# A Mamba layer and a mixture of experts in one kernel: weights fetched apart from token rows, the scan one projection later, counts per block of 512, the optional blocks ahead of the last two

## The chip, the cores and the metric

The kernel runs on one core of one Trainium2 chip. The metric is the device time of one execution in microseconds. TensorE (PE) does the matmuls, VectorE (DVE), ScalarE (ACT) and GpSimd (POOL) everything elementwise, and transfers are issued from the queues of SyncE (SP), ACT and POOL. PEld is PE's weight load, which overlaps its matmuls.

## The reference

4096 tokens of 256 features pass through two layers, each with a residual and a layer norm. The first is a Mamba block (512 inner channels, convolution over 4 tokens, 16 states, a scan over all tokens), the second a mixture of 8 experts that sends each token to one of them.

```python
xz = input_tensor @ W_in                      # 256 -> 2 * 512
conv_in, gated = xz[..., :512], xz[..., 512:]
convolved = silu(causal_conv(conv_in, conv_w) + conv_b)
x_dbl = convolved @ W_x                       # delta, B, C
delta = softplus(x_dbl[..., :1])
h = exp(delta * A) * h + delta * B * convolved[..., :16]     # scan over tokens
y = sum(h * C) + convolved * D_param
x = layernorm(x + (y * silu(gated)) @ W_out)

e = argmax(x @ Wr.T + br)                     # one expert for each token
x = layernorm(x + relu(x @ W1[e].T + b1[e]) @ W2[e].T + b2[e])
```

## The kernel before

**The Mamba part** goes in NB = 8 chunks of TB = 512 tokens, JT = 4 tiles of 128 each. Step k of the main loop issues the eight projections of chunk k (`project(k, 0)` to `project(k, 7)`, tile `pm`, L477, 128 columns of W_in each), and between them the later stages of the chunks a = k-1, b = k-2 and c = k-3. ACT evicts the first four to `xc` and `acc` (L484, L486), DVE convolves (L490), and ACT applies silu (L482, L493). Chunk a gets `gauge` (px, L502), `gauge_out` (pxo, and a long DVE chain to `sr`, L515 to L546), `look_out` and `scan` (pt, L554, then exp, scan and `hC`, to L565). Chunk b gets `gate` (py, L572), `project_out` in four tiles (po, L612) and `choose`, in which the expert is found and the tokens of each expert are counted (`earlier`, L666). Chunk c gets `rank` (pr, L677 and L680: each token's place within its expert), `blocks_of` and `place` (rowh, colh and pz, L703 to L717: lists of the tokens by place).

**The table.** Sorted by expert, the tokens make blocks of 128. At most NSB = 39 blocks are needed; the first SURE = 37 always run. `blocks_of` calls `table` after chunks 2, 4, 5 and 7, which set up blocks 0 to 4, 5 to 12, 13 to 16 and 17 to 38. It computes which expert a block belongs to (`widx`, L294) and returns a function `lookup`. This one reads the token numbers out of the lists (pi, L306; `tidx`, L313) and is called later, by `tokens_of`, once the lists are placed.

**An expert block** (`blocks`, a generator that yields after each quarter) has these pieces. `fetch` issues two indirect transfers from POOL: the 128 token rows `xg` (L352, 128 KB, four buffers) and the expert's whole weights `we` (L357, 2.23 MB, three buffers), for blocks up to AHEAD = 2 ahead. `turn` transposes the rows (pg L376, copy `xgT` on DVE, L380). `hidden` makes each half of the hidden layer (ph L392; relu by ACT, L400, for the first, and by DVE, L402, for the second). `close` does the second matmul in halves (pe L414), adds `xs` = xg + b2 (L421) and the result (`r`, L423), the layer norm (L217 to L224) and an indirect write from POOL (`out`, L426). The generator `quarters` runs over blocks 0 to 36, and `expert(n)` takes n quarters of it. `fill` says how many after each projection in the steps k = 6 and 7; behind the loop calls of `expert` alternate with the last stages, and then the rest runs. The last two blocks stand in a conditional (L840) that compares a number read from the table; the profiled execution doesn't take it.

**What sets the order.** PE's order is that of the code, written by hand. The other engines' order is the framework's scheduler's. PSUM banks are shared by tag: three for pm, px and ph (`mm`), two for transposes and small results (`tr`), and those for py, po and pe (`o`). The weights of the router are prepared by `router_weights` (pw L336, pwo L344), called in step 0.

Of the kernel before, what the change touches and what calls it, by code (L numbers as in the profile page):

```python
# [33 lines left out]
F32 = mybir.dt.float32  # L34
# [4 lines left out]
ALU = mybir.AluOpType  # L39
# [40 lines left out]
def mamba_moe(  # L80
# [53 lines left out]

    load(0)
    win = const.tile([P, DC, 2 * DI], F32, name="win")
    for at in (slice(0, DI), slice(DI, 2 * DI)):
        nc.sync.dma_start(win[:, 0, at], W_in[0:P, at])
        nc.scalar.dma_start(win[:, 1, at], W_in[P : 2 * P, at])
        if at.start == 0:  # L140
            cw = const.tile([P, CC, KC], F32, name="cw")
            nc.scalar.dma_start(cw, conv_w.rearrange("(c p) k -> p c k", p=P))
            cb = const.tile([P, CC], F32, name="cb")
            nc.sync.dma_start(cb, conv_b)
# [83 lines left out]

    index = {}

    taken = const.tile([P, NE], F32, name="taken")

# [4 lines left out]
    def table(b0, nb, columns, rows, early):  # L239
# [52 lines left out]
        nc.vector.tensor_scalar(eb, eb, float(NE - 1), float(P), ALU.min, ALU.mult)  # L292
        widx = const.tile([P, nb], I32, name=f"widx{b0}")
        nc.vector.tensor_scalar(widx, eb, part, None, ALU.add)  # L294
        if early:

            left = small("left", [NE])
            nc.vector.tensor_scalar(left, starts, -1.0, float(nb * P), ALU.mult, ALU.add)
            nc.vector.scalar_tensor_tensor(left, left, 0.0, whole, ALU.max, ALU.min)
            nc.vector.tensor_tensor(taken, taken, left, ALU.add)  # L300

        def lookup():

            pi = bank("tr", f"pi{b0}", 2)
            for h in range(LH):
                nc.tensor.matmul(  # L306
                    pi[:, 0:nb], lhsT=lists[:, h * P : (h + 1) * P], rhs=pick[:, h, :],
                    start=(h == 0), stop=(h == LH - 1),
                )
            half = small("half", [nb])  # L310
            nc.vector.tensor_scalar(half, pi[:, 0:nb], 0.0, -float(T + 1), ALU.is_gt, ALU.mult)
            tidx = const.tile([P, nb], I32, name=f"tidx{b0}")
            nc.vector.scalar_tensor_tensor(tidx, pi[:, 0:nb], float(T), half, ALU.add, ALU.add)  # L313
            for b in range(nb):
                index[b0 + b] = rows, widx[:, b : b + 1], tidx[:, b : b + 1]

        return lookup

# [28 lines left out]
                )  # L347
        nc.scalar.copy(wout[:, :, D : D + NE], pov)

    def fetch(b):  # L350
        xg = m3.tile([P, D], F32, tag="xg", name=f"xg{b}", bufs=4)
        nc.gpsimd.indirect_dma_start(  # L352
            out=xg, out_offset=None, in_=x1d[0 : index[b][0], :],
            in_offset=bass.IndirectOffsetOnAxis(ap=index[b][2], axis=0),
        )
        we = m3.tile([P, WROW], F32, tag="we", name=f"we{b}")
        nc.gpsimd.indirect_dma_start(  # L357
            out=we, out_offset=None, in_=experts,
            in_offset=bass.IndirectOffsetOnAxis(ap=index[b][1], axis=0),
        )  # L360
        return xg, we

    fetched, turned, hid, open_ = {}, {}, {}, {}

    current = 0

    def prefetch(b):
        for ahead in range(b, min(b + AHEAD, (SURE if b < SURE else NSB) - 1) + 1):
            if ahead in index and ahead not in fetched:
                fetched[ahead] = fetch(ahead)  # L370

    def turn(b):

        px = bank("tr", f"pg{b}", 2)
        for dc in range(DC):
            nc.tensor.transpose(  # L376
                px[:, dc * P : (dc + 1) * P], fetched[b][0][:, dc * P : (dc + 1) * P], ident
            )
        turned[b] = m2.tile([P, DC * P], F32, tag="xgT", name=f"xgT{b}")
        nc.vector.tensor_copy(turned[b], px[:, 0 : DC * P])  # L380

    def hidden(b, half):
        we, xgT = fetched[b][1], turned[b]
        if half == 0:
            hid[b] = m2.tile([P, FC, P], F32, tag="hT", name=f"hT{b}")
        hT = hid[b]
        ph = bank("mm", f"ph{b}_{half}")
        fcs = range(half * FC // 2, (half + 1) * FC // 2)
        for n, fc in enumerate(fcs):
            for dc in range(DC):  # L390
                at = dc * FF + fc * P
                nc.tensor.matmul(  # L392
                    ph[:, n * P : (n + 1) * P], lhsT=we[:, at : at + P],
                    rhs=xgT[:, dc * P : (dc + 1) * P],
                    start=(dc == 0), stop=(dc == DC - 1),
                )
        for n, fc in enumerate(fcs):
            bias = we[:, OB + fc : OB + fc + 1]
            if half == 0:
                nc.scalar.activation(hT[:, fc, :], ph[:, n * P : (n + 1) * P], AF.Relu, bias=bias)  # L400
            else:
                nc.vector.tensor_scalar(  # L402
                    hT[:, fc, :], ph[:, n * P : (n + 1) * P], bias, 0.0, ALU.add, ALU.max
                )

    def close(b, half):
        xg, we = fetched[b]
# [18 lines left out]
        nc.gpsimd.indirect_dma_start(  # L426
            out=out, out_offset=bass.IndirectOffsetOnAxis(ap=index[b][2], axis=0),
            in_=y[:, 0, :], in_offset=None, bounds_check=T - 1, oob_is_err=False,
        )

    def blocks(*span):

        nonlocal current
        turn_next = True
        for b in range(*span):
            current = b
            prefetch(b)
            if turn_next:
                turn(b)
            hidden(b, 0)  # L440
            yield
            hidden(b, 1)
            yield
            turn_next = b + 1 not in fetched
            if not turn_next:
# [195 lines left out]
    def choose(i):  # L641
# [19 lines left out]
        nc.vector.tensor_reduce(best, lg, AX.X, ALU.max)  # L661
        oh = a2.tile([P, JT, NE], BF16, tag="oh", name=f"oh{i}")
        nc.vector.tensor_tensor(oh, by_token(back), by_expert(best), ALU.is_equal)
        for j in range(JT):
            at = i * JT + j
            nc.vector.tensor_tensor(  # L666
                earlier[:, at + 1, :], earlier[:, at, :], oh[:, j, :], ALU.add
            )
        st[i]["oh"], st[i]["best"] = oh, best

    def rank(i):
# [5 lines left out]
        nc.tensor.matmul(  # L677
            prv, lhsT=trib, rhs=oh.rearrange("p j e -> p (j e)"), start=True, stop=False
        )
        nc.tensor.matmul(  # L680
            prv, lhsT=oneb,
            rhs=earlier[:, i * JT : (i + 1) * JT, :].rearrange("p j e -> p (j e)"),
            start=False, stop=True,
        )
        rk = a2.tile([P, JT, NE], F32, tag="rk", name=f"rk{i}")
        nc.vector.tensor_tensor(
# [37 lines left out]

    def blocks_of(i):

        done = len(index)
        if i + 1 in EARLY:
            lookups[i] = table(done, EARLY[i + 1] - done, (i + 1) * JT, (i + 1) * TB, True)
# [8 lines left out]
    def have(i):  # L738
        return 0 <= i < NB
# [5 lines left out]
    for k in range(NB):  # L745
# [53 lines left out]
    tokens_of(c - 1)  # L799
    expert(2)  # L800
    gauge_out(a)
    expert()
# [84 lines left out]
```

## Time and profile before

| what | us |
|---|---|
| median of 3 runs (lowest, highest) | 566.27 (565.71, 566.81) |
| the profiled execution's own time | 564.27 |
| its span in the profile | 562.4 |
| PE busy | 507.1 |
| DVE, ACT, POOL busy | 349.1, 226.0, 174.3 |
| bytes moved by DMA | 106.92 MB, of which 91.65 MB on POOL's software queue |
| mean granted PE clock | 0.963 of full speed |

By stage, PE busy of the time: 20.2 of the first 30.0 us; 26.9 of 30 to 60; 111.9 of 60 to 180; 13.1 of 180 to 200, where the first expert block starts; 92.4 of 200 to 300 and 55.8 of 300 to 360, where expert blocks and the last Mamba stages are mixed; 179.6 of 360 to 540, expert blocks alone; 7.2 of the last 22.4.

The profile's page gives each engine's busy time and its state in 40 slices of the span. The waits are the idle times of an engine, sorted by what ended them. The timeline gives single instructions with their start and duration; in square brackets stands how long the engine was idle before, and what released it. Records of matmuls overlap, so their lengths don't add up. A line number is that of the kernel before.

### The profile page before, as it was taken

The page shows a single profiled execution, that of the slowest core. Times are in us where ns is not written, and L with a number is a line of the kernel's source. Part 1 is how long each engine was busy: PE and PEld are TensorE (multiplying, and loading weights), DVE is VectorE, ACT ScalarE, POOL GpSimd, SP SyncE. Part 2 cuts the span into 40 slices and gives each one's busy share as a digit, 9 for nine tenths or more (in the row PEclk, how much of TensorE's full clock was granted, in tenths as well). Part 3 has the DMA queues.
Part 4 walks back from the last instruction along what each step waited for, and adds up shares of the span by engine and source line. Part 5 has one row for each costly group of instructions (what it writes and reads, how often), then busy time and mean ns, then how long its engine had stood idle before and what let it go on. Part 6 is the DMA issues. An engine that isn't in the chain of part 4 may idle for free. (4 is left out here: it accounts for less than half of the span.)

```text
span 562.4 us, 7855 instructions
## 1 busy us (share of the span) xinstructions
PE 507.1 (90%) x2754; PEld 385.9 (69%) x2754; DVE 349.1 (62%) x1171; ACT 226.0 (40%) x462; POOL 174.3 (31%) x191
## 2 busy tenths in 40 slices
PE   4897999898989599989969898999999999999990
PEld 1533454545454377567659787998999999999980
DVE  0446879786898827876858968444544445554440
ACT  2358576776676526575523211111111111111110
POOL 2000303333244531332432512323333444444210
PEclk9699999998999789989989999999999999999996
DMA  9110103030309704604545856888999999989900
GB/s 264 41 38 1 38 1 112 2 112 1 113 1 361 272 4 169 233 10 169 180 141 195 305 210 226 316 318 314 352 336 340 343 345 343 336 337 358 339 28 0
DMA packets 22729, 106.92 MB, mean 190 GB/s; under 512 B 4222, under 2 KB 12929, under 8 KB 17954
## 3 DMA queue, kind: packets, MB, share of 16 engines
q0 software_dynamic: 8880, 91.65, 43.7%
q1 hardware_dynamic: 10928, 12.85, 7.3%
q10 hardware_dynamic: 2882, 1.93, 1.2%
q8 instruction: 22, 0.36, 0.3%
q14 instruction: 17, 0.14, 0.1%
HBM read 98.02 MB, written 9.04 MB: 190 GB/s over the span
## 5 line engine op out<-in xcount | busy, mean ns | idle before, releaser
L392 PEld LDWEIGHTS ph<-xgT,we 128*128 128x128 f32 x1184 | 140.3, 194 | 8.9 <-DVE xgT L380 3.2
L392 PE MATMUL ph<-xgT,we 128*128 128x128 f32 x1184 | 141.7, 277 | 4.7 <-DVE xgT L380 2.4
L414 PE MATMUL pe<-we,hT 128*128 128x256 f32 x592 | 136.7, 382 | 0.4 <-DVE hT L402 0.4
L477 PE MATMUL pm<-xTb,win 128*128 128x512 f32 x256 | 126.1, 630 | 8.8 <-DMA win<-in_W_in 7.0
L414 PEld LDWEIGHTS pe<-we,hT 128*128 128x128 f32 x592 | 110.1, 192 | 15.6 <-DVE hT L402 1.3
L477 PEld LDWEIGHTS pm<-xTb,win 128*128 128x128 f32 x256 | 49.8, 202 | 63.0 <-issue 53.1
L490 DVE SCALAR_TENSOR_TENSOR acc<-xc,cw,acc 128x512 f32<-128x512 f32 x96 | 71.3, 787 | 16.0 <-ACT acc L486 15.5
L221 ACT ACTIVATE sdm<-sdm 128x1 f32<-128x1 f32 x37 | 7.5, 203 | 183.0 <-DVE sdm L220 182.9
L426 POOL DMA_INDIRECT out<-y,tidx x37 | 37.6, 1016 | 104.6 <-DVE hT L402 53.6
L612 PE MATMUL po<-wout,sg 128*128 128x264 f32 x256 | 65.4, 400 | 0.0
L357 POOL DMA_INDIRECT we<-in_experts,widx x37 | 36.3, 981 | 77.5 <-PE pe L414 39.7
L400 ACT ACTIVATE hT<-ph,we 128x128 f32<-128x128 f32 x148 | 42.7, 368 | 38.3 <-issue 19.8
L402 DVE TENSOR_SCALAR hT<-ph,we 128x128 f32<-128x128 f32 x148 | 42.6, 343 | 23.9 <-PE ph L392 23.6
L612 PEld LDWEIGHTS po<-wout,sg 128*128 128x128 f32 x256 | 47.4, 194 | 9.4 <-POOL xc L471 1.8
L423 DVE TENSOR_TENSOR r<-pe,xs 128x256 f32<-128x256 f32 x37 | 15.7, 423 | 56.4 <-PE pe L414 56.3
L578 POOL TENSOR_TENSOR sg<-cv,sg 128x512 f32<-128x512 f32 x22 | 29.7, 1376 | 54.2 <-DVE earlier L666 38.7
L352 POOL DMA_INDIRECT xg<-x1d,tidx x37 | 36.5, 986 | 31.5 <-PE pg L376 12.2
L616 DVE TENSOR_TENSOR xb<-po,xb 128x264 f32<-128x264 f32 x32 | 13.7, 427 | 32.6 <-PE po L612 32.1
L703 POOL TENSOR_SCALAR rowh<-lrow,row,code 128x256 f16<-128x256 bf16 x20 | 25.1, 1264 | 24.9 <-DVE col L699 13.8
L574 DVE SCALAR_TENSOR_TENSOR cv<-cv,dp,py 128x512 f32<-128x512 f32 x32 | 23.5, 738 | 9.5 <-PE py L572 9.5
L482 ACT ACTIVATE sg<-pm 128x512 f32<-128x512 f32 x32 | 19.1, 595 | 25.5 <-PE pm L477 25.3
L421 DVE TENSOR_TENSOR xs<-xg,we 128x256 f32<-128x256 f32 x37 | 15.4, 415 | 22.1 <-DMA we<-in_experts,widx 15.3
(151 smaller groups left out, 512.7 us busy)
## 6 DMA issues: line engine op xcount, KB each, us to landing
xb<-in_x SPq DMA_DIRECT2D x8, 512.0 KB, 6.1
x1d<-x SPq DMA_DIRECT2D x8, 512.0 KB, 5.2
xTb<-in_xT SPq DMA_DIRECT2D x7, 512.0 KB, 3.6
we<-in_experts,widx POOLq DMA_INDIRECT x37, 9.8
xg<-x1d,tidx POOLq DMA_INDIRECT x37, 5.0
out<-y,tidx POOLq DMA_INDIRECT x37, 6.1
win<-in_W_in ACTq DMA_DIRECT2D x2, 256.0 KB, 6.1
win<-in_W_in SPq DMA_DIRECT2D x2, 256.0 KB, 6.3
```

The source lines that it names most:

```text
L352: nc.gpsimd.indirect_dma_start(out=xg, out_offset=None, in_=x1d[0 : index[b][0], :], in_offset=bass.IndirectOffsetOnAxis(ap=index[b][2], a ...
L357: nc.gpsimd.indirect_dma_start(out=we, out_offset=None, in_=experts, in_offset=bass.IndirectOffsetOnAxis(ap=index[b][1], axis=0),)
L392: nc.tensor.matmul(ph[:, n * P : (n + 1) * P], lhsT=we[:, at : at + P], rhs=xgT[:, dc * P : (dc + 1) * P], start=(dc == 0), stop=(dc == DC ...
L400: nc.scalar.activation(hT[:, fc, :], ph[:, n * P : (n + 1) * P], AF.Relu, bias=bias)
L402: nc.vector.tensor_scalar(hT[:, fc, :], ph[:, n * P : (n + 1) * P], bias, 0.0, ALU.add, ALU.max)
L414: nc.tensor.matmul(py[:, 0:D], lhsT=hT[:, fc, :], rhs=we[:, at : at + D], start=(fc == 0), stop=(fc == FC - 1),)
L426: nc.gpsimd.indirect_dma_start(out=out, out_offset=bass.IndirectOffsetOnAxis(ap=index[b][2], axis=0), in_=y[:, 0, :], in_offset=None, boun ...
L477: nc.tensor.matmul(pm, lhsT=win[:, dc, c * P : (c + 1) * P], rhs=xTb[:, dc, :], start=(dc == 0), stop=(dc == DC - 1),)
L490: nc.vector.scalar_tensor_tensor(acc, xc[:, c, k : k + TB], cw[:, c, k : k + 1], acc, ALU.mult, ALU.add)
L578: eng.tensor_tensor(sg[:, c, :], cv[:, c, :], sg[:, c, :], ALU.mult)
L612: nc.tensor.matmul(po[:, 0 : D + NE], lhsT=sg[:, c, j * P : (j + 1) * P], rhs=wout[:, c, :], start=(c == 0), stop=(c == CC - 1),)
L703: (nc.vector if i >= NB - 3 else nc.gpsimd).tensor_scalar(rowh[:, j, :], lrow, row[:, j : j + 1], code[:, i * JT + j : i * JT + j + 1], AL ...
```

## The change

1. W_in is loaded in three slices of columns (128, 384 and 512) instead of two, each still in two halves on SP and ACT.
2. `earlier` holds counts per chunk and not per tile of 128. `choose` makes one reduction and one addition instead of four additions; `rank` adds up the tiles within a chunk by three more matmuls.
3. `fetch` is gone. `prefetch` issues the rows of a block once `tidx` is known and the weights once `widx` is known, and is also called at the end of `blocks_of`.
4. `xs` may be issued only after the last relu of its block.
5. `router_weights` is called in step 1, behind `gauge`.
6. `scan` stands behind projection 6, `place` ahead of it, and `tokens_of` of chunk c at the end of its own step. `fill` has other numbers: 8 and 10 quarters instead of 7 and 9.
7. `quarters` runs to block 34; the conditional comes next, and blocks 35 and 36 stand behind it. The spare blocks share one weight buffer. `turn` is skipped for a block that is turned already.

```diff
-    for at in (slice(0, DI), slice(DI, 2 * DI)):
+    for at in (slice(0, P), slice(P, DI), slice(DI, 2 * DI)):
...
-    earlier = const.tile([P, NT + 1, NE], BF16, name="earlier")
+    earlier = const.tile([P, NB + 1, NE], BF16, name="earlier")
...
     def prefetch(b):
-        for ahead in range(b, min(b + AHEAD, (SURE if b < SURE else NSB) - 1) + 1):
-            if ahead in index and ahead not in fetched:
-                fetched[ahead] = fetch(ahead)
+        for n in range(b, min(b + AHEAD, SURE - 1) + 1) if b < SURE else (b,):
+            if n in index and n not in xgs:
+                xgs[n] = m3.tile([P, D], F32, tag="xg", name=f"xg{n}", bufs=4)
+                nc.gpsimd.indirect_dma_start(
+                    out=xgs[n], out_offset=None, in_=x1d[0 : index[n][0], :],
+                    in_offset=bass.IndirectOffsetOnAxis(ap=index[n][1], axis=0),
+                )
+            if n in weights and n not in wes:
+                wes[n] = (
+                    wes[SURE] if n > SURE else m3.tile([P, WROW], F32, tag="we", name=f"we{n}")
+                )
+                nc.gpsimd.indirect_dma_start(
+                    out=wes[n][:, :], out_offset=None, in_=experts,
+                    in_offset=bass.IndirectOffsetOnAxis(ap=weights[n], axis=0),
+                )
...
-        nc.vector.tensor_tensor(xs, xg, we[:, OC : OC + D], ALU.add)
+        with tc.issue_after(last[b].ins):
+            nc.vector.tensor_tensor(xs, xg, we[:, OC : OC + D], ALU.add)
...
-            if turn_next:
+            if b not in turned:
                 turn(b)
...
-    quarters = blocks(0, SURE)
+    quarters = blocks(0, SURE - 2)
...
-        for j in range(JT):
-            at = i * JT + j
-            nc.vector.tensor_tensor(
-                earlier[:, at + 1, :], earlier[:, at, :], oh[:, j, :], ALU.add
-            )
+        here = a2.tile([P, NE], F32, tag="here", name=f"here{i}")
+        nc.vector.tensor_reduce(here, oh.rearrange("p j e -> p e j"), AX.X, ALU.add)
+        nc.vector.tensor_tensor(earlier[:, i + 1, :], earlier[:, i, :], here, ALU.add)
...
+        for n in range(JT - 1, 0, -1):
+            nc.tensor.matmul(
+                prv[:, n * NE :], lhsT=oneb, rhs=ohr[:, 0 : (JT - n) * NE], start=False, stop=False
+            )
...
-            lookups[i] = table(done, NSB - done, NT, T + 1, False)
+            lookups[i] = table(done, NSB - done, NB, T + 1, False)
+        prefetch(current)
...
-        fill = {NB - 2: (0, 0, 0, 1, 2, 2, 2), NB - 1: (1, 1, 1, 1, 2, 2, 1)}.get(k, (0,) * 7)
+        fill = {NB - 2: (0, 1, 1, 1, 1, 2, 2), NB - 1: (1, 1, 1, 2, 1, 2, 2)}.get(k, (0,) * 7)
         project(k, 0)
         if have(b):
             gate(b)
-        if have(c - 1):
-            tokens_of(c - 1)
...
-        if k == 0:
+        if k == 1:
             router_weights()
...
         look(k)
+        if have(b):
+            project_out(b, 2)
+        if have(c):
+            place(c)
+        expert(fill[5])
+        project(k, 6)
         if have(a):
             scan(a)
-        if have(b):
-            project_out(b, 2)
-        expert(fill[5])
-        project(k, 6)
-        if have(c):
-            place(c)
...
         project(k, 7)
+        if have(c):
+            tokens_of(c)
...
     with tc.If(held[0] > (SURE - EARLY[6]) * P, preferred_fallthrough_block=False):
         for _ in blocks(SURE, NSB):
             pass
+    for _ in blocks(SURE - 2, SURE):
+        pass
```

More of the change, by code (lines that the diff above doesn't have):

```diff
@@ L227, in layernorm @@
             )
-    index = {}
+    index, weights = {}, {}
     taken = const.tile([P, NE], F32, name="taken")
@@ L294, in table @@
         nc.vector.tensor_scalar(widx, eb, part, None, ALU.add)
+        for b in range(nb):
+            weights[b0 + b] = widx[:, b : b + 1]
         if early:
@@ L314, in lookup @@
             for b in range(nb):
-                index[b0 + b] = rows, widx[:, b : b + 1], tidx[:, b : b + 1]
+                index[b0 + b] = rows, tidx[:, b : b + 1]
         return lookup
@@ L348, in router_weights @@
         nc.scalar.copy(wout[:, :, D : D + NE], pov)
[L350 to L354, printed above, removed]
-        )
[L356 to L363, printed above, removed]
+    xgs, wes, turned, hid, last, open_ = {}, {}, {}, {}, {}, {}
     current = 0
     def prefetch(b):
-        for ahead in range(b, min(b + AHEAD, (SURE if b < SURE else NSB) - 1) + 1):
-            if ahead in index and ahead not in fetched:
-                fetched[ahead] = fetch(ahead)
+        for n in range(b, min(b + AHEAD, SURE - 1) + 1) if b < SURE else (b,):
[13 more added lines that the diff above has]
+                )
     def turn(b):
@@ L376, in turn @@
             nc.tensor.transpose(
-                px[:, dc * P : (dc + 1) * P], fetched[b][0][:, dc * P : (dc + 1) * P], ident
+                px[:, dc * P : (dc + 1) * P], xgs[b][:, dc * P : (dc + 1) * P], ident
             )
-        turned[b] = m2.tile([P, DC * P], F32, tag="xgT", name=f"xgT{b}")
+        turned[b] = (
+            turned[SURE] if b > SURE else m2.tile([P, DC * P], F32, tag="xgT", name=f"xgT{b}")
+        )
         nc.vector.tensor_copy(turned[b], px[:, 0 : DC * P])
     def hidden(b, half):
-        we, xgT = fetched[b][1], turned[b]
+        we, xgT = wes[b], turned[b]
         if half == 0:
@@ L401, in hidden @@
             else:
-                nc.vector.tensor_scalar(
+                last[b] = nc.vector.tensor_scalar(
                     hT[:, fc, :], ph[:, n * P : (n + 1) * P], bias, 0.0, ALU.add, ALU.max
@@ L406, in close @@
     def close(b, half):
-        xg, we = fetched[b]
+        xg, we = xgs[b], wes[b]
         hT = hid[b]
@@ L426, in close @@
         nc.gpsimd.indirect_dma_start(
-            out=out, out_offset=bass.IndirectOffsetOnAxis(ap=index[b][2], axis=0),
+            out=out, out_offset=bass.IndirectOffsetOnAxis(ap=index[b][1], axis=0),
             in_=y[:, 0, :], in_offset=None, bounds_check=T - 1, oob_is_err=False,
@@ L433, in blocks @@
         nonlocal current
-        turn_next = True
         for b in range(*span):
@@ L443, in blocks @@
             yield
-            turn_next = b + 1 not in fetched
-            if not turn_next:
+            if b + 1 in xgs:
                 turn(b + 1)
@@ L663, in choose @@
         nc.vector.tensor_tensor(oh, by_token(back), by_expert(best), ALU.is_equal)
-        for j in range(JT):
-            at = i * JT + j
-            nc.vector.tensor_tensor(
-                earlier[:, at + 1, :], earlier[:, at, :], oh[:, j, :], ALU.add
-            )
+        here = a2.tile([P, NE], F32, tag="here", name=f"here{i}")
+        nc.vector.tensor_reduce(here, oh.rearrange("p j e -> p e j"), AX.X, ALU.add)
+        nc.vector.tensor_tensor(earlier[:, i + 1, :], earlier[:, i, :], here, ALU.add)
         st[i]["oh"], st[i]["best"] = oh, best
@@ L679, in rank @@
         )
+        ohr = oh.rearrange("p j e -> p (j e)")
+        for n in range(JT - 1, 0, -1):
+            nc.tensor.matmul(
+                prv[:, n * NE :], lhsT=oneb, rhs=ohr[:, 0 : (JT - n) * NE], start=False, stop=False
+            )
         nc.tensor.matmul(
-            prv, lhsT=oneb,
-            rhs=earlier[:, i * JT : (i + 1) * JT, :].rearrange("p j e -> p (j e)"),
-            start=False, stop=True,
+            prv.rearrange("p (j e) -> p j e", e=NE), lhsT=oneb,
+            rhs=earlier[:, i, :].unsqueeze(1).to_broadcast([P, JT, NE]), start=False, stop=True,
         )
@@ L725, in blocks_of @@
     def blocks_of(i):
-        done = len(index)
+        done = len(weights)
         if i + 1 in EARLY:
-            lookups[i] = table(done, EARLY[i + 1] - done, (i + 1) * JT, (i + 1) * TB, True)
+            lookups[i] = table(done, EARLY[i + 1] - done, i + 1, (i + 1) * TB, True)
         elif i == NB - 1:
-            lookups[i] = table(done, NSB - done, NT, T + 1, False)
+            lookups[i] = table(done, NSB - done, NB, T + 1, False)
+        prefetch(current)
     def tokens_of(i):
@@ L798, in mamba_moe @@
     gauge(a)
-    tokens_of(c - 1)
     expert(2)
```

## The prediction

> **What bounds the kernel now.** I read the page first, for who is busy.
>
> ```profile
> PE 507.1 (90%) x2754; PEld 385.9 (69%) x2754; DVE 349.1 (62%) x1171; ACT 226.0 (40%) x462; POOL 174.3 (31%) x191
> PEclk9699999998999789989989999999999999999996
> ```
>
> TensorE (PE) sets the time: 507.1 of 562.4 us busy, so 55.3 us is all that can be had without removing matmuls, besides busy time spent at a low clock (the 6, the 7 and the 8s of the clock row). Nothing in the change removes matmuls, so I sort the idle time. PE's waits come next: line, what it waited for, total us, times, longest.
>
> ```profile
> PE pg L376 <- DMA xg<-x1d,tidx: 11.7, 2, 6.4
> PE pt L554 <- DVE sr L546: 8.9, 4, 3.1
> PE pm L477 <- DMA win<-in_W_in: 7.0, 1, 7.0
> PE ph L392 <- DVE xgT L380: 2.4, 2, 1.9
> PE ph L392 <- DVE col L699: 2.3, 1, 2.3
> PE pn L249 <- ACT sr L523: 1.9, 1, 1.9
> PE pm L477 <- ACT hT L400: 1.9, 1, 1.9
> PE pw L336 <- DMA wr<-in_WrT: 1.4, 1, 1.4
> PE pwo L344 <- DMA woutT<-in_W_outT: 1.4, 1, 1.4
> ```
>
> These are 38.9 us. The tail, 547.2 to 562.4, is 15.2 more. Each row has a place in the timeline, and the change touches nearly all of them. At the start (start us, length, engine):
>
> ```profile
> 6.97 6.23 PE L477 MATMUL pm<-xTb,win 128*128 128x512 f32 x8 [6.97 <-DMA win<-in_W_in]
> 12.09 0.59 ACT L484 COPY xc<-pm 128x512 f32<-128x512 f32 x1
> 14.63 0.58 PE L336 MATMUL pw<-wr,ones 128*128 128x8 f32 x4 [1.43 <-DMA wr<-in_WrT]
> 16.61 3.58 PE L344 MATMUL pwo<-wr,woutT 128*128 128x8 f32 x16 [1.39 <-DMA woutT<-in_W_outT]
> 20.04 2.91 PE L477 MATMUL pm<-xTb,win 128*128 128x512 f32 x3
> ```
>
> PE waits for W_in, does two of chunk 0's eight projections, waits twice for the router's weights, and is then at half clock. The stages with that clock, in the table by windows (PE busy, PEld, DVE, ACT, POOL, granted clock, DMA share, GB/s):
>
> ```profile
> 190.00:194.00 4.00, 0.25 (x2) 0.28 (x2) 1.85 (x11) 2.90 (x4) 0.00 (x0) 0.50 0.47 184
> 194.00:198.00 4.00, 3.48 (x16) 3.08 (x16) 3.71 (x21) 0.00 (x0) 3.08 (x3) 0.50 0.14 41
> 285.00:289.00 4.00, 3.11 (x10) 2.63 (x11) 2.30 (x11) 0.00 (x0) 0.94 (x1) 0.57 0.24 67
> ```
>
> So a long stall costs twice. The first one (PE idle 187.4 to 193.7) comes from POOL's timeline:
>
> ```profile
> 167.62 1.20 POOL L357 DMA_INDIRECT we<-in_experts,widx  x1 [0.18 <-DVE mva L621]
> 169.12 0.94 POOL L357 DMA_INDIRECT we<-in_experts,widx  x1 [0.30 <-issue]
> 181.52 1.41 POOL L357 DMA_INDIRECT we<-in_experts,widx  x1
> 183.23 1.12 POOL L352 DMA_INDIRECT xg<-x1d,tidx  x1 [0.30 <-issue]
> ```
>
> The token rows (xg0) leave after three weight sets of 2.23 MB and land at 193.6, just after the third set (193.1). From 360 to 540 us PE is busy 20.0 of every 20 us: a block is 7.7 us there and nothing in the change shortens it.
>
> [...]the matmul records are 0.86 us at the start and 0.43 later; stalls of 6.4 and 5.3 us were followed by 0.50 to 0.57. [...]xg0's landing 0.5 us after we2's, 10.4 us after its own issue[...] (alone it takes 2.7 to 2.9). [...]In the trace PE's next instruction after the branch over the spare blocks came 0.3 us later[...]. [...]the four adds of L666: 0.15 us alone, 0.65 to 0.72 beside POOL work, 403 ns in the mean.
>
> **The change part by part.** The sum is against the profiled execution, 564.3 us (span 562.4 plus 1.9); the median of the runs is 2.0 above it.
>
> *Start.* The first slice of W_in is 64 KB per half, so 0.64 MB lies ahead of the first matmul instead of 1.02. At the 215 to 300 GB/s of those microseconds this is 1.3 to 1.8 us: PE starts near 5.3. It costs one more DMA issue on SP and on ACT (0.35 to 0.45 us each). With pw/pwo gone to chunk 1, projections run on; the clock rises near 10.4 instead of 25. The three PSUM banks fill before ACT's first eviction, which I leave at 12.1 to 12.6: ACT issues DMAs and loads a table until then. After it ACT needs 1.15 us for a pair and PE 1.88 us a projection at full clock: five after 13.3 end near 23 to 24.4 instead of 33.9. That is -9.5. pw and pwo return at full clock: 4.2 us at half becomes +2.2. Net -7; -3 if PE's wait for the third bank (1 to 2 us) cools it again, -9 at best.
>
> *Scan after projection 6.* pt now stands behind po_2 (1.95), pm_6 (1.88) and, with the ranking of an older chunk, pz (0.61). The four waits (3.1, 1.4, 2.2, 2.2) are shorter than 4.4 us, so they go. What is late next is py at the next chunk's start: from pt to hC took 5.9 us at 105.02 to 110.91, and py came 3.9 us after that. pt starts 2.2 us later against PE's own work, so the slack becomes about -0.6 to +1.3: I return 0.6 us in five chunks and 0.4 elsewhere: -5.5. The stall at 134 also left a clock of 0.63 for 4 us (1.5 us), of which I count 1.0: net -6.5; between 0 (py waits take it all) and -10.
>
> *Counts.* Three more bf16 matmuls per chunk; two such records start 0.03 us apart, and full-width ones would take 0.1: 24 x 0.03 to 0.1 = +0.7 to +2.4, I take +1.0. DVE gives up two of four adds (0.8 us a chunk), hidden under PE; without that cover it would only help. The smaller memset is at the start on POOL and hidden.
>
> *Weights at table time, first block earlier.* Counted from pr (155.1): widx comes at +10, we0 leaves at +12.5 behind the four rowh (5 us). Now we1 and we2 follow at once, as three buffers are free: 6.7 MB at the 345 GB/s of the steady stage plus up to 1.5 MB of loads put their end, and xg0's, at +35 to +37 (before: +38.5). But PE reaches pg0 at +27.9 (pm_7 ends +20.6, then pi, pm_0, py, pm_1, px) instead of +32.3. Stall 7 to 9 us instead of 6.4: +0.7 to +2.7, I take +1.5. The second stall (5.3, at 285.9): xg leaves right behind tidx, and pi no longer waits for the next chunk's gate. It becomes some 3.3 us and may not cool PE: -2.5 (0 to -5). The 1.9 us of pm on hT at 240 and the half clock after it (2.1 us) need not recur with another fill: -2, between +1 and -4.
>
> *xs late.* xgT copies stood behind DVE's add, which waited 15.3 us for weights in all[...]: -1.5 (0 to -2). The add itself (0.42) lies under the 3.6 us of close; without that cover it would cost 0.42 x 37.
>
> *Branch two blocks earlier.* PE's ph of block 35 takes a bank last used in the skipped body by DVE, so PE waits until DVE has finished y34 and its own branch: r to y took 547.26 to 549.43, so +2.6 with the branch (up to +4). Queued behind it are only PE's own last two blocks, so it is paid in full. Block 36 turns a stale block 37: +0.4.
>
> *End.* After PE's last matmul come r, y, the write, its landing and the final barrier, as now. POOL's rows at the end hold a semaphore update at the branch (L840, 2.4 us) and then a 9.1 us DRAIN (L883, 552.4 to 561.6). The update moves under block 35. The DRAIN goes along only if the update causes it; at the kernel's beginning the same update was followed by a DRAIN of 0.17 us, so I leave it where it is: 0, with -9 as the other end.
>
> Sum: -7 -6.5 +1 +1.5 -2.5 -2 -1.5 +2.6 +0.4 = -14.0, so 550.3 for a profiled execution and **552.3 us** as the median.
>
> **Rivals.**
> *The DRAIN belongs to the branch* (chance 0.22). For it: it follows the update directly, and nothing else runs on POOL then. Against: it may be the closing of all software DMAs, of which 111 went before. Then 552.3 - 9 = 543.
>
> *The Mamba stage hands its gains back* (0.18). From 60 to 180 us DVE is busy 102 of 120 us, and PE comes earlier to the same results: py waits take the 6.5, and the third bank cools PE at the start (-3). Left: -3 +1 +1.5 -2.5 -2 -1.5 +2.6 +0.4 = -3.5, so 562.8.
>
> *Weights ahead of rows, slower* (0.10). At all four tables three weight sets may stand in the ring ahead of the first row. Each costs 2.23 MB / 340 GB/s = 6.6 us. If each table's stall grows by one set, 4 x 6.6 = 26 against gains of 14: 566.3 + 12 = about 578; it decides from 14 us in all, 3.5 a table. [...]Against: at later tables the buffers are in use, so at most one set can be fetched at once, and blocks lie between.
>
> **How the numbers follow.** My sum has 0.50, the rivals 0.22, 0.18 and 0.10. The sum's own range, with its ends mixed, is 545 to 558. With 2 in 10 left out, the cases reach from 541 (DRAIN gone) to 563. The runs of before lie within 0.2% of their median, which is about what can be told from no change. Faster: all of the first two, most of the third: 0.87. Same 0.04, slower 0.09.
>
> **What would show it.** PE's first matmul near 5.3 us, chunk 0's last projection near 24, no half clock from 16 to 26. No pt waits; py waits of at most 1 us. xg0's stall 7 to 9 us. A PE gap of 2.6 us two blocks before the end, on DVE. The last DRAIN of POOL 9 us or gone. I am wrong if pt's total returns at py, or if the xg waits together pass 20 us.

## The result: half a per cent, where 2.5 were forecast

The changed kernel takes 563.72 us in the median of 20 runs (560.52 to 567.11), the kernel before 566.37 in 20 runs beside it: 0.9952 of before, 95% interval 0.9929 to 0.9976. It is faster, clear of the noise but by under 1%: some 3 us instead of 14, and 0.7 us above the upper end of the forecast, 563. Its profiled execution spans 562.0 us against 562.4. Two of the seven executions of one later kernel (place and conditional both moved back) were in a slow state, at 800 and 1342 us, and are left out of its figures.

The page of the changed kernel, its row of engines and its clock:

```profile
PE 508.3 (90%) x2780; PEld 385.7 (69%) x2780; DVE 344.7 (61%) x1156; ACT 223.8 (40%) x461; POOL 174.7 (31%) x191
PEclk9989999899979699999979999999999999999997
```

PE is as busy as before, and its clock as low in the mean (0.965 against 0.963). The half clock has left the start; it stands near the end of the Mamba stage (0.50 from 156 to 160 us) and at the first block (0.50 from 188 to 192). PE's waits in the changed kernel (line, what it waited for, total us, times, longest):

```profile
PE pg L378 <- DMA xg<-x1d,tidx: 5.1, 1, 5.1
PE pm L481 <- DMA win<-in_W_in: 5.1, 1, 5.1
PE ph L396 <- ACT cv L497: 4.4, 1, 4.4
PE pg L378 <- DVE cv L578: 4.2, 1, 4.2
PE pz L723 <- POOL rowh L709: 3.9, 4, 1.0
PE pn L249 <- ACT sr L527: 3.3, 1, 3.3
PE pm L481 <- ACT acc L490: 3.1, 2, 2.8
...
PE pr L679 <- DVE oh L667: 2.5, 3, 0.8
PE ph L396 <- DVEq L847: 2.3, 1, 2.3
PE pe L418 <- DVE hT L406: 1.5, 2, 1.1
PE py L576 <- DVE hC L569: 0.9, 1, 0.9
PE pt L558 <- DVE sr L550: 0.6, 1, 0.6
```

Nearly every row of before is gone or smaller (pn's has grown, from 1.9 to 3.3), and rows that weren't there have taken their place: pz on POOL's rowh, pr on the choice of the chunk before, pm on ScalarE, ph behind the conditional, and pe for 2.6 us at 347 us, where ph had waited 2.3. From 30 to 180 us PE's waits in the two timelines add up to 11.2 us before (pt 3.12 + 1.40 + 2.17 + 2.23 + 0.41, pn 1.88) and 11.1 after (pt 0.60, py 0.85, pr 0.84 + 0.83 + 0.78, pz 4 x 0.97, pn 3.31). The time of 60 to 180 us by windows, of before and after, shows that the clock fell, too (columns as in the prediction):

```profile
60.00:180.00 120.00, 111.92 (x434) 61.72 (x435) 101.81 (x317) 86.42 (x138) 38.48 (x35) 0.99 0.22 75
```

```profile
60.00:180.00 120.00, 110.02 (x422) 61.04 (x420) 91.42 (x296) 79.05 (x126) 34.97 (x33) 0.96 0.24 86
```

The start of px, once in a chunk, shows where a lead is lost. It began at 37.6 us (chunk 0), 60.2, 88.3, 117.7, 148.9 and 179.1 (chunk 5) before, and at 29.6, 55.1, 82.0, 114.5, 145.4 and 180.1 after. The lead of 8.0 us at chunk 0 is 1.0 us of delay at chunk 5. Of these 9.0 us, 3.1 go between chunks 2 and 3, and 4.6 between chunks 4 and 5. In the latter stretch stands pn, the first matmul of the table. ScalarE's last copy out of pxo and PE's pn behind it, after and before:

```profile
155.90 0.19 ACT L527 COPY sr<-pxo 128x64 f32<-128x64 f32 x1
156.14 0.17 PE L249 MATMUL pn<-earlier,oneb 128*128 128x8 bf16 x1 [3.31 <-ACT sr L527]
```

```profile
156.92 0.23 ACT L523 COPY sr<-pxo 128x64 f32<-128x64 f32 x1
157.20 0.17 PE L249 MATMUL pn<-earlier,oneb 128*128 128x8 bf16 x1 [1.88 <-ACT sr L523]
```

In the code px, pxo, pr and pn take the two `tr` banks in turn (px does not stand in `mm`, as the description of the kernel before has it), so pn needs the bank that ScalarE empties with this copy. ScalarE starts it 4.1 us after pxo's matmuls end, where it took 1.6 before; ahead of it stand, among others, a table load (1.28 us at 151.7, after a wait of 1.17) and silu (at 155.4, after 0.47), which waited for VectorE's convolution. Behind pn the clock is 0.50 from 156 to 160 us and 0.85 to 164, where it was 1.00 before. No run moves this wait alone, so its cause is read from trace and code and not shown.

### The profile page after: what moved, and what is told of

Its sections match the earlier page's. It is cut to its first block, busy times and chain, and to the rows that moved or that the text cites. A ratio compares the mean times of both kernels' runs of the same rounds, so it can differ in the third digit from the quotient of the medians.

```text
span 562.0 us, 7926 instructions
## 1 busy us (share of the span) xinstructions
PE 508.3 (90%) x2780; PEld 385.7 (69%) x2780; DVE 344.7 (61%) x1156; ACT 223.8 (40%) x461; POOL 174.7 (31%) x191
## 3 DMA queue, kind: packets, MB, share of 16 engines
q0 software_dynamic: 8880, 91.65, 43.8%
## 5 line engine op out<-in xcount | busy, mean ns | idle before, releaser
L494 DVE SCALAR_TENSOR_TENSOR acc<-xc,cw,acc 128x512 f32<-128x512 f32 x96 | 78.3, 838 | 18.8 <-ACT acc L490 18.2
L488 ACT COPY xc<-pm 128x512 f32<-128x512 f32 x32 | 18.5, 578 | 18.9 <-PE pm L481 18.6
```

What stands on the lines that cost most here:

```text
L494: nc.vector.scalar_tensor_tensor(acc, xc[:, c, k : k + TB], cw[:, c, k : k + 1], acc, ALU.mult, ALU.add)
```

## The experiments

Each kernel was timed beside the kernel before. Ratios are to that kernel, with 95% intervals.

**Was it the move of place?** Theory A says that place, put ahead of projection 6, makes PE wait for POOL; theory B that VectorE and ScalarE set the pace of this stage anyway. The timeline of the changed kernel, on PE and on POOL:

```profile
99.41 0.28 PE L723 MATMUL pz<-colh,rowh 128*128 128x128 f16 x2
100.65 0.23 PE L723 MATMUL pz<-colh,rowh 128*128 128x128 f16 x1 [0.97 <-POOL rowh L709]
101.85 0.45 PE L723 MATMUL pz<-colh,rowh 128*128 128x128 f16 x5 [0.97 <-POOL rowh L709]
102.14 2.69 PE L481 MATMUL pm<-xTb,win 128*128 128x512 f32 x4
...
96.87 4.92 POOL L709 TENSOR_SCALAR rowh<-lrow,row,code 128x256 f16<-128x256 bf16 x4 [5.50 <-DVE col L705]
```

POOL makes the four rowh one after the other, 1.2 us each, and pz asks for them 1.9 us sooner than when projection 6 lay between. The projection behind takes 2.69 us instead of 1.88: the clock is down.

```diff
             project_out(b, 2)
-        if have(c):
-            place(c)
         expert(fill[5])
         project(k, 6)
         if have(a):
             scan(a)
+        if have(c):
+            place(c)
```

> The changed kernel with one edit: place of the older chunk stands behind projection 6 and the scan again, not ahead of it. Theory A (the move of place cost what the move of the scan brought: the list matmuls wait for POOL's four rowh, 3.9 us in four waits, and the clock falls to 0.82 and 0.84 behind them): these waits go, the clock stays at 1.00 from 100 to 110 us, px of chunk 5 comes 4 to 6 us earlier than its 180.1 us, and the time is 0.7 to 1.0% below that of the changed kernel. Theory B (from 60 to 180 us VectorE and ScalarE set the pace and TensorE only changes the place where it waits): waits of 3 to 4 us appear at pr, pn, pt or py instead, px of chunk 5 moves by less than 1.5 us and the time by less than 0.2%.

Measured: 556.74 us, 0.9825 (0.9785 to 0.9865), so 1.3% below the changed kernel, more than theory A expected. px of chunk 5 starts at 171.9 instead of 180.1; 1.0 us of this lead was there at chunk 2, before the first place, so 7.2 us belong to the stretch with place. pz waits no more:

```profile
100.03 0.60 PE L558 MATMUL pt<-ident,sr 128*80 128x128 f32 x4
100.47 0.75 PE L723 MATMUL pz<-colh,rowh 128*128 128x128 f16 x8
101.06 2.00 PE L616 MATMUL po<-wout,sg 128*128 128x264 f32 x8
```

As a whole, the stage was not paced by the other engines. The move of place cost 7 us: 3.9 us of waits, and behind the first two of the four a clock of 0.82 and 0.84 from 100 to 110 us, about 1.7 us more (an estimate from these clocks). Behind the other two, at 133.2 and 134.4 us, the clock stayed at 1.00, so some 1.6 of the 7.2 us are not traced. Not all waits went: pr's three for the choice (2.4 us) and pn's 3.31 are still there. This kernel is the base of what follows.

**The scan alone, on the kernel before.**

```diff
         look(k)
-        if have(a):
-            scan(a)
...
         project(k, 6)
+        if have(a):
+            scan(a)
         if have(c):
             place(c)
```

> The kernel before with one edit: scan behind projection 6 (place stays behind projection 6, too). Theory A: the waits of pt, 8.9 us, fall below 2 us, nothing takes their place, px of chunk 5 comes 5 us or more before its 179.1 us; the time is 0.8 to 1.2% below before. Theory B: pt's waits turn into waits at py, pr or pn, px of chunk 5 moves by less than 2 us and the time by less than 0.4%.

Measured: 566.33 us, 0.9994 (0.9972 to 1.0017), px of chunk 5 at 184.7: theory A's numbers fail here. Of theory B's, the time and the new waits came, but px moved by 5.6 us, and later. pt's waits fall to 1.2 us, and PE's list of waits has new rows:

```profile
PE pr L680 <- DVE earlier L666: 6.7, 4, 2.0
...
PE pr L677 <- DVE oh L663: 2.5, 3, 0.8
```

With a later scan, VectorE comes later to the choice of experts, and from there each of its small steps is issued between two convolution steps of 0.74 us. pr needs the first three of the four additions to `earlier`, and these end after PE asks for them: at 126.6 and 128.8 us it waits 0.84 and then 2.01, and the clock of 60 to 180 us is 0.94. So the counts per chunk should matter. They take two of the four steps away, and more: with them pr reads only the counts up to the chunk before, and the chunk's own tiles come from three matmuls on the choice. In the changed kernel pr's last matmul, at 152.66 us, comes ahead of the addition at 153.84. That was tested on the base:

```diff
-        here = a2.tile([P, NE], F32, tag="here", name=f"here{i}")
-        nc.vector.tensor_reduce(here, oh.rearrange("p j e -> p e j"), AX.X, ALU.add)
-        nc.vector.tensor_tensor(earlier[:, i + 1, :], earlier[:, i, :], here, ALU.add)
+        for j in range(JT):
+            at = i * JT + j
+            nc.vector.tensor_tensor(
+                earlier[:, at + 1, :], earlier[:, at, :], oh[:, j, :], ALU.add
+            )
... (rank with two matmuls, as before)
```

> The base with the counts of the kernel before (four additions per chunk, two matmuls in rank). With the scan moved alone, pr's second matmul waited 2.01 us for the fourth addition in three chunks, besides 0.83 for the choice. If the additions are what the counts edit takes off the path: these 2.01 us waits come back three times or more, the clock falls behind them, px of chunk 5 comes 5 us or more after the base's 171.9, the time 1% or more above the base. If the counts edit is neutral: no such waits, less than 0.2%.

Measured: 564.71 us, 0.9971 (0.9940 to 1.0001), 1.5% above the base; px of chunk 5 at 178.0, 6.1 us later. PE's list of waits shows the wait back:

```profile
PE pr L684 <- DVE earlier L670: 6.0, 3, 2.0
```

So with the later scan the new counts are worth 8 us. What the scan's move is worth with them isn't shown: the new counts without the move weren't tried.

**The start alone, on the kernel before.**

```diff
-    for at in (slice(0, DI), slice(DI, 2 * DI)):
+    for at in (slice(0, P), slice(P, DI), slice(DI, 2 * DI)):
...
-        if k == 0:
+        if k == 1:
             router_weights()
```

> The kernel before with the two edits of the start alone: W_in in three slices, the router's weights in step 1. Both theories: first matmul near 5.1 us, the first px near 29.6 instead of 37.6. Theory A: the lead of 5 to 8 us stays up to chunk 5 (px near 173 to 174), and the time is 0.8 to 1.2% below before. Theory B: pt's waits grow from 8.9 to 12 us or more, px of chunk 5 is within 2 us of 179.1, and the time within 0.4% of before.

Measured: 560.63 us, 0.9906 (0.9870 to 0.9942). px of chunk 0 starts at 29.6, of chunk 1 at 55.9 (4.4 ahead), of chunk 5 at 177.6 (1.5 ahead), and the profiled execution ends 3.5 us earlier. Neither theory has all its numbers. The time is theory A's, but the lead it expected up to chunk 5 is not there; px of chunk 5 is theory B's, but pt's waits stay at 8.3 us in four, and they do not grow. Of the lead, 2.6 us go to pw and pwo, which now stand between chunks 0 and 1; the rest shrinks where the clock is lower (0.83 against 1.00 from 40 to 50 us, 0.96 against 0.99 from 60 to 180). The start is worth 5.6 us by the times.

Why not 7 or more? The timeline of ScalarE in the changed kernel:

```profile
11.19 0.45 ACTq L158 DMA_DIRECT2D wr<-in_WrT  x1
13.14 0.35 ACTq L160 DMA_DIRECT2D brb<-in_br  x1
...
14.81 0.20 ACT L167 ACTIVATE nega<-al 16x1 f32<-16x1 f32 x1
14.92 0.56 ACT L488 COPY xc<-pm 128x512 f32<-128x512 f32 x1
```

The first eviction comes at 14.9 us, not at 12.1: ScalarE's queue is longer in issuing transfers (its last issue is at 14.16, before at 11.65), and PE waits 2.8 us for a bank at 16.2. To test that, the later loads were issued from POOL, and `nega` was computed in step 1:

```diff
-    nc.scalar.dma_start(wout[:, :, 0:D], ...)
+    nc.gpsimd.dma_start(wout[:, :, 0:D], ...)
... (also wr, brb, the row of zeros in x1d, woutT)
-    nc.scalar.activation(nega, al, AF.Exp)
-    nc.vector.tensor_scalar(nega, nega, -1.0, None, ALU.mult)
...
         if k == 1:
+            nc.scalar.activation(nega, al, AF.Exp)
+            nc.vector.tensor_scalar(nega, nega, -1.0, None, ALU.mult)
             router_weights()
```

> The base with ScalarE freed at the start: the loads of W_out, the router's weights and bias, W_outT and the row of zeros are issued from POOL, and the exponential of A_log (nega) is taken in step 1. If ScalarE's own queue makes its first eviction late (14.9 us in the changed kernel, 12.1 before): it starts near 8 to 9 us, TensorE's wait of 2.8 to 3.2 us at 15 to 16 us falls below 0.5, px of chunk 0 comes 2.5 to 4 us before 30.2, and 2 to 4 us of it reach the end. If the evictions wait for something else, the first stays after 11 us.

Measured: 544.98 us, 0.9638 (0.9601 to 0.9676), against 0.9825 for the base. PE doesn't wait for a bank any more, and chunk 0's first six projections run in one stretch:

```profile
5.20 12.17 PE L479 MATMUL pm<-xTb,win 128*128 128x512 f32 x24 [5.20 <-DMA win<-in_W_in]
```

The first eviction starts at 8.6 us, px of chunk 0 at 24.9 (base: 30.2, so 5.3 earlier, where 2.5 to 4 were expected), and the last write of results is issued 3.4 us earlier (538.7 against 542.1), as expected. But the profiled span is 10.6 us shorter. The other 7 us come from the end and are taken up below.

**The conditional's place.**

```diff
-    quarters = blocks(0, SURE - 2)
+    quarters = blocks(0, SURE)
...
     with tc.If(held[0] > (SURE - EARLY[6]) * P, preferred_fallthrough_block=False):
         for _ in blocks(SURE, NSB):
             pass
-    for _ in blocks(SURE - 2, SURE):
-        pass
```

> The changed kernel with the conditional behind block 36 again, as before. If TensorE's gap there (2.32 us) and the turn of a stale block (0.4 us) are the whole price on TensorE, its last matmul ends 2.7 us earlier than 548.5. If POOL's last DRAIN runs 9 us from the end of whatever software DMA work comes last, it ends 10.8 us after the last write was issued instead of 9.1, so the span is 1.0 us shorter than the changed kernel's. If the branch cost more than its gap, 3 us or more shorter; if its place is free, no difference.

Measured: 560.42 us, 0.9884 (0.9842 to 0.9926). In its profile PE's last result is taken up (`r`) at 542.1 instead of 548.5, 6.4 us earlier; 3.6 of these it was ahead at block 35's transposes already, 2.6 of them since chunk 1, far ahead of anything that the edit moves. 2.8 us are the conditional's. From the issue of the last write to the end it takes 12.7 us, in the changed kernel 11.0. So the place costs 2.8 and returns 1.7, by one profile of each kernel; the times, which also hold the luck of the clock (a mean of 0.962 to 0.969 in its six runs), can't show the 1.1 us that remain. Together with place:

> The changed kernel with its two losing moves undone: place behind projection 6 again, the conditional behind block 36 again. If the two add up: 1.3% for place, and TensorE's 2.7 us less the DRAIN's 1.7 us for the branch: span near 552, time 0.972 to 0.982 of before. If they share a cause, no better than place alone (0.9825).

Measured: 555.25 us, 0.9820 (0.9774 to 0.9865), which can't be told from the base alone (0.9825).

**The first expert block.** In the changed kernel pg waits 4.16 us and ph then 4.37 (in the base 5.30 and 3.23). In the changed kernel both waits are named after instructions whose results they don't read, so the cause is another. The timeline of VectorE and POOL has two candidates:

```profile
180.52 4.89 DVE L494 SCALAR_TENSOR_TENSOR acc<-xc,cw,acc 128x512 f32<-128x512 f32 x1
...
190.72 0.42 DVE L384 COPY xgT<-pg 128x256 f32<-128x256 f32 x1
```

```profile
181.13 3.72 POOL L582 TENSOR_TENSOR sg<-cv,sg 128x512 f32<-128x512 f32 x3
```

One convolution step of VectorE takes 4.89 us instead of 0.74 while POOL does three products in a row (3.72 us). And xgT, which ph needs, comes at 190.7, far behind pg. Theory C holds VectorE to be late, theory D the weights ahead in the queue. First, chunk 4's products all on VectorE:

```diff
-            eng = nc.vector if c == CC - 1 or (c % 2 and i >= NB - 2) else nc.gpsimd
+            eng = nc.vector if c == CC - 1 or i == NB - 4 or (c % 2 and i >= NB - 2) else nc.gpsimd
```

> The changed kernel with place moved back (call it the base: span 553.1, first block: pg waits 5.30 for its rows, ph waits 3.23), and chunk 4's four gating products all on VectorE instead of three on POOL. In the base one VectorE instruction at 172.1 takes 4.30 us instead of 0.16 while POOL does three products in a row, and xgT stands behind it. Theory C (ph waits for xgT because VectorE is blocked by POOL's products): the wait of ph falls from 3.2 to 1.5 or less, pg keeps its 5.3; time 0.2 to 0.5% below the base. Theory D (the weights in the queue are the whole cause, VectorE is not): both waits stay within 0.5 us.

Measured: 556.89 us, 0.9817 (0.9777 to 0.9858), no gain in time. The long step of VectorE (4.30 us in the base) is gone. ph's wait falls from 3.23 to 2.15 us, less than theory C asked and more than theory D allowed, and pg's from 5.30 to 4.14; px of chunk 5 to the first ph takes 8.9 instead of 11.1 us. Then, only the first set of weights ahead of the rows:

```diff
-            if n in weights and n not in wes:
+            if n in weights and n not in wes and (n not in (1, 2) or n in rowdma):
...
+                with (tc.issue_after(rowdma[n].ins) if n in (1, 2) else nullcontext()):
                     nc.gpsimd.indirect_dma_start(out=wes[n][:, :], ...)
```

> The base with only one set of weights ahead of the first rows at the first table: the queue is we0, xg0, xg1, we1, xg2, we2. Theory C: pg's wait (5.3) goes or falls below 1 us, but ph then waits 6 us or more for xgT, as VectorE is as busy as ever; the first ph starts less than 2.5 us earlier relative to px of chunk 5 (base: 171.9 to 183.0, 11.1 us). Theory D: first ph 4 to 5 us earlier in that measure and the time 0.7% below the base. Either way a later block may wait for its weights, at 12 us or so behind.

Measured: 555.82 us, 0.9817 (0.9774 to 0.9859), again no gain in time. The first pg waits no more (5.30 us in the base), and ph waits 6.95 us where the two together had 8.53. PE's ph, and VectorE's copy ahead of it:

```profile
179.24 3.75 PE L399 MATMUL ph<-xgT,we 128*128 128x128 f32 x16 [6.95 <-issue]
```

```profile
178.72 0.41 DVE L387 COPY xgT<-pg 128x256 f32<-128x256 f32 x1
```

px of chunk 5 to the first ph is 9.3 us. So the rows had been late by the queue, as the prediction had it, and behind them stood a second cause of nearly the same size. Both edits together:

> The base with both edits (gating on VectorE for chunk 4, one set of weights ahead). Theory C: px of chunk 5 to first ph shrinks from 11.1 to 4 to 6 us, the half clock behind it goes, the time is 1.0 to 1.5% below the base. Theory D: as with one set of weights ahead alone.

Measured: 553.17 us, 0.9770 (0.9726 to 0.9814), 8.1 us from px to ph: the hoped for 4 to 6 weren't reached, and the time is 0.6% below the base, not 1.0 to 1.5. ph still waits 5.82 us, since the four products now stand on VectorE ahead of xgT (at 178.2). The long step beside POOL's products was a part (without it ph's wait had fallen from 3.23 to 2.15); the rest should be the queue of ready work ahead of the copy. To test that, ScalarE made block 0's copy, with one set of weights ahead and the products on POOL as in the base:

```diff
-        nc.vector.tensor_copy(turned[b], px[:, 0 : DC * P])
+        (nc.scalar.copy if b == 0 else nc.vector.tensor_copy)(turned[b], px[:, 0 : DC * P])
```

> The base with one set of weights ahead, and block 0's xgT copied by ScalarE instead of VectorE. With one set ahead, pg was not late any more, but ph waited 6.95 us; xgT's copy stood behind 6.5 us of other VectorE work issued ahead of it. Theory C' (VectorE's queue of ready work, not the block by POOL alone, keeps xgT): ph's wait falls to 1.5 us or less, px of chunk 5 to first ph shrinks from 9.2 to 3 to 4.5 us, time 0.5 to 1.0% below that kernel (0.973 to 0.977 of before). If ph waits for its weights instead, ph's wait stays at 5 us or more.

Measured: 549.56 us, 0.9710 (0.9673 to 0.9747). px to ph takes 4.1 us, and ph waits 1.81 (a little more than expected, behind ScalarE's own work). So it was VectorE that kept xgT, by its queue of ready work and the long step beside POOL's products together (theory C').

**All edits together.**

> All of it: place and the conditional back, one set of weights ahead, chunk 4's products on VectorE, xgT of block 0 on ScalarE, ScalarE freed at the start. Each alone, from runs and estimates: 7 us for place, 1 for the branch, 4 to 6 for the first block, 2 to 4 for the start. If they add, 545 to 550 us, 0.960 to 0.970 of before; if the gains shift into other waits, above 0.972.

Measured: 534.14 us, 0.9449 (0.9406 to 0.9492), 11 us below the lower end of what was expected. Most of that is again at the end: from the issue of the last write to the end it takes 3.8 us, in the kernel before 12.7. It is faster than both kernels.

**What happened at the end?** POOL's last DRAIN, as the line of the kernel's end has it (shortest, median and longest in ns, then first and last start), in the kernel before, and in the one with ScalarE freed at the start:

```profile
L883 POOLq DRAIN  x3: 45/107/9147, 552.4 to 562.2; - x3
```

```profile
L892 POOLq DRAIN  x3: 51/109/2920, 538.5 to 542.2; - x3
```

Three single edits of the kernel before ask which of the loads on POOL does it; each has one `nc.scalar.dma_start` turned into `nc.gpsimd.dma_start`.

> The kernel before with one 4 KB load (the router's bias) issued from POOL instead of ScalarE. The prediction left POOL's last DRAIN (9.15 us in every kernel so far, 10.4 with the conditional ahead) as fixed; with five loads issued from POOL at the start it was 1.9 and 2.9. Theory E (any direct load on POOL's queue takes the long DRAIN away): DRAIN 2 to 3 us, the span 6 us shorter, 0.989 of before. Theory F (it goes with how much or how many are issued): DRAIN between 7 and 9.

> The kernel before with one 512 KB load (W_out) issued from POOL. Theory E: as with the bias, DRAIN 2 to 3 us. Theory F (bytes or descriptors): shorter than with the bias alone, but not the whole 7 us.

> The kernel before with the 1 KB row of zeros (SBUF to the table of rows in HBM) written from POOL's queue. Theory E: DRAIN 2 to 3 us. Theory F: 9 us, as only one row moves.

Measured: the bias 566.66 us, 0.9980 (0.9957 to 1.0003), DRAIN 9.22 us; the row of zeros 567.16 us, 0.9986 (0.9964 to 1.0009), DRAIN 9.23; W_out 556.96 us, 0.9774 (0.9744 to 0.9805), with this DRAIN:

```profile
L883 POOLq DRAIN  x3: 51/109/1837, 553.1 to 555.8; - x3
```

From the issue of the last write to the end it takes 12.7 us in the kernel before and 3.5 with W_out on POOL: 9.2 of the 10.9 us between the medians of these two (the kernel before took 567.82 beside it). Theory E falls, as a small load does nothing. Theory F had the row of zeros right, but not the rest: 32 packets more (8912 against 8880 on the software queue) lengthen the DRAIN by 0.08 us, and 144 more (9024) take 7.3 us off, not in proportion. The semaphore update at the conditional falls with it, from 2.43 to 0.36 us. What in the queue's state decides it stays open, and the other two loads of the earlier edit (W_r and W_outT) weren't tried alone.

## Why the prediction was wrong, by its own steps

| step | forecast, us | found, us | from |
|---|---|---|---|
| start | -7 | -5.6 (-7.4 to -3.3) | start alone |
| scan behind projection 6 | -6.5 | 0, alone | scan alone |
| place ahead of it | in the 4.4 us of cover | +7 | place back |
| counts | +1.0 | -8 on the base | old counts |
| first block | stall 7 to 9 | 4.16 + 4.37 = 8.5 | profile |
| second stall | -2.5 | -0.2 | profile |
| pm on hT at 240 us | -2 | -1.9 idle | profile |
| xs late | -1.5 | about -0.4 | profile |
| conditional | +2.6 + 0.4 | +2.8 | branch at end |
| DRAIN and update | 0 | -1.7 | branch at end |

The figures found don't add up to the 2.65 us measured: each holds beside the other edits of its run.

**The step that failed is "Scan after projection 6".** It counted "pz (0.61)" as work that covers pt, by its length alone. pz was moved, too, and what it waits for wasn't looked at: four rowh of POOL, which end 4.9 us after they begin. Place back alone brought 7 us. That the waits of pt would go was right (8.9 to 0.6 us), and so was the bound on py (0.85).

**A second error lies in the same step: the chain was followed to hC and no further.** VectorE does the scan, then the choice; the choice came later, and pr waits for it. That made the scan alone worth nothing. For the same reason **the step "Counts"** had the wrong sign. It priced the matmuls (that was right: the five records of pr begin within 0.12 us), and held VectorE's saving to be hidden, which it was before and is not with the later scan. It didn't see that the new rank no longer waits for the additions of its own chunk.

The rival "the Mamba stage hands its gains back" came nearest in time (562.8), and the sum of idle time from 30 to 180 us is what it says (11.2 and 11.1). That closeness is in part luck, as its sum has the start at -3 and place at nothing. Its mechanism was wrong: py took 0.85 us and not 6.5, and the stage as a whole was not bound by VectorE, since one edit takes pz's waits away and px of chunk 5 comes 8.2 us earlier. A part of it is true: pr waits for VectorE's choice (2.5 us in three), pn for ScalarE, which had waited for VectorE (3.31), and both stay in the base. The rival on the slower side, weights ahead of rows, is shown at the first table only, and in part; the two long waits for rows, 4.16 and 5.12 us, are far from 20 together. The DRAIN doesn't belong to the branch: with the conditional two blocks earlier it is still there, and takes 10.37 us.

**Start.** The mechanism was right; the term "which I leave at 12.1 to 12.6" was mis-sized: 14.9. PE started at 5.10 us, as forecast, and with ScalarE free the first eviction is at 8.6.

**First block.** The size was right and the cause half right: rows late by the queue (4.16), then xgT late on VectorE (4.37). **Second stall.** The rows left 1.9 us earlier (278.2 against 280.1), but between pi and pg PE has 3.4 us of work now and had 5.1, so it comes as much earlier and waits as long. The step looked at the transfer and not at when PE asks for it. **xs late**: the wait of 1.92 us at 317.7 (before it, a product on VectorE took 2.43 us at 314.2, beside one of POOL, and the next, at 317.6, took 0.67) went, and pe's waits for hT of 1.12 and 0.42 came, the first behind a product on VectorE of 2.89 us at 319.5.

**Conditional**: right: 2.32 us and the turned stale block. What wasn't seen is that the update of 2.4 us no longer stands between the last write and the DRAIN.

## What to carry to other kernels

When a stage is moved so that it covers another's wait, treat every instruction of it as one that can wait: look up when its inputs are ready, on each engine, and follow the engine's queue past the chain that one had in view. An edit that seems only to save instructions on a hidden engine can become the one that counts once another edit delays that engine: ask also which waits it cuts. And when a wait is named after an instruction that had long ended, test it by moving one input at a time: behind the transfer stood a copy that was just as late.

## What the runs showed of the hardware that was not expected

POOL's last DRAIN is 9.15 us in the kernel before, with its end 12.7 us after the last write was issued. With one 512 KB load of W_out issued from POOL at the start it is 1.84 us, and the kernel 2.3% faster (0.9774). A 4 KB or 1 KB transfer there leaves it at 9.2. The conditional's place doesn't shorten it (10.37 us ahead of the last two blocks, of which the first 1.2 lie before and under the last write).

Equal waits of PE were not followed by equal clocks. Two waits of 0.97 us each were followed by 0.82 and 0.84 at 100 us and by 1.00 at 134 us, in the same execution. In the kernel before, a wait of 1.88 us was followed by 1.00 at 157 us and by 0.60 at 240 us, and one of 3.12 us at 48.5 us left it at 1.00. A clock of 0.60 over 4 us costs some 1.6 us (an estimate: 0.40 of the 4 us), so two single profiles can differ by as much in one stage with the same waits. What decides the clock isn't shown by these runs.
